# Three batches instead of four in the first output class, and four small moves in a two-layer mixture kernel

## The chip, the cores and the metric

The kernel runs on one core of one Trainium2 chip. The time is the device time of one execution, in microseconds (us); of several executions the median is given. On the core five engines work side by side, each with its own queue of instructions: TensorE (PE, matrix products; its weight loads are listed apart as PEld), VectorE (DVE), ScalarE (ACT), GpSimd (POOL) and SyncE (SP, which here issues nearly all DMAs). They wait for each other by semaphores.

## The reference, cut to what matters

```python
def kernel_reference(x, ...):                         # x: [8 batches, 256 tokens, 128]
    # layer 0: pooled = attention pooling of x, in 16 groups of 128 tokens
    logits = einsum('bld,ed->ble', pooled, gate_weight)              # 8 experts
    gates  = logits * (logits >= kth smallest of all logits)
    h = gelu_tanh(einsum('bld,ehd->bleh', pooled, w1) + b1)          # H = 512
    x = x + sum over e of gates_e * (einsum('bleh,edh->blde', h, w2) + b2)   # every token, every expert

    # layer 1, conditioning: one adapter for the language of each batch
    h = relu(x @ W1[lang] + b1[lang])                                # 128 -> 32
    z = x + h @ W2[lang] + b2[lang]                                  # 32 -> 128
    z = layernorm(z) * gamma[lang] + beta[lang]
    # layer 1, mixture: each token goes to 2 of 8 experts
    xn = layernorm(z) * gamma + beta
    w, idx = top_k(softmax(xn @ gate_w), 2);  w = w / sum(w)
    out = sum over its 2 experts of w_e * (gelu(xn @ w1_e + b1_e) @ w2_e + b2_e)
    return x + out + z
```

All of it is float32. There are 2048 tokens, 16 tiles of 128 (`NT = 16`); a batch is two tiles.

## The kernel before, in words

**Layer 0.** The tokens go in units, `UNITS = [(0,0,4), (1,0,4), (2,0,4), (3,0,2), (3,2,2)]`: group, offset and number of tiles. Units 0 to 2 have four tiles (`nt == GT`, 512 columns), units 3 and 4 two (256 columns). In `layer`, for each unit and expert, TensorE makes the hidden products `hp_first` (L945, four chunks, each evicted with the gelu by ScalarE, L947, into `hT_first`) and, one expert behind, the output products `yp_first` (L925). VectorE multiplies by the gates (`part_first`, L913) and adds up (`acc_first`, L915). Each product is 128 columns of weights, and as the operands are float32 each product takes two matmul records (passes) in a trace.

**The adapter and the routing of layer 1 run inside layer 0.** When the eighth expert of a unit is added up, `adapt(u, acc)` is queued in `behind`. It is a generator: `pump()`, called after each chunk of products (with 256 columns after every second), steps the first generator of the queue to its next `yield`. So where a product of `adapt` stands in TensorE's queue is set by the number of yields before it. In order, `adapt` does:

- `x2T`, the sum with x; `fp` (L566), transposes to rows of tokens, and `x2`;
- `adp` (L705): W1 of the adapter, two products, one for each half of the unit, into partitions 0 to 31 and `LANE` to `LANE + 31` of one tile (`LANE` is 64; `A` is 32); `ha` (L707): VectorE adds the bias, a column of the tile `las[u]`, and takes the relu, one operation for each half;
- `dp` (L715): W2, contracting over 33 rows (32 and a row of ones for the bias), alternating between the halves; `xr` (L720), the sum;
- the two layernorms (`normed`, with `ve` and `rstd` on VectorE and GpSimd), `zr`, the rows to be sent, `znp` (L749) transposes, and the gate: `l1q` (L763), the gate product in four blocks of 32 partitions, `l1p` (L770, L775);
- the top two by `top_one`, and `sofar`, running sums over the unit's tiles of how many tokens chose each expert (L802);
- `kp` (L808, L809): two products that turn the sums into each token's place among its expert's rows; then `at`, `wh`, `pos`, and GpSimd's indirect DMAs (L830), which scatter the tokens with their weights to the sorted rows `xs` in DRAM, eight for a unit of four tiles, four for one of two.

**The experts of layer 1.** Sorted rows go in tiles of 128, k = 0 to 35 (`SURE`) and up to three more under a runtime condition. After units 2, 3 and 4 a list (`listed`) says which tile holds which rows of which expert (`SLOTS = {2: 17, 3: 21, 4: 39}`): tiles 0 to 16 can begin once unit 2 is placed, 17 to 20 after unit 3, 21 on after unit 4. For a tile: `xt` is loaded, transposed (`xtp`, L1019, evicted as `xc`, L1021), the hidden products `hps` (L1034, gelu `hs`, L1036), output products `yps` (L1043), `yt` (L1047), which applies the token's weight, and an indirect DMA to `ys` (L1050). The last four tiles (`PLACED = 32` on) are not scattered: they are added for the last two batches by one-hot products `late` (L1106).

**The classes.** Within a list the tiles are sorted in three classes (`CLASSES`), by what their rows' batches are: those that hold rows of the first `FIRST = 4` batches come first, then those of the first `EARLY = 6`, then the rest. `holding` counts, from `kp`, how many tiles are full of the early ones. So the outputs of batches 0 to `FIRST - 1` are settled after tile `SETTLED_FIRST - 1` (k = 28) and those up to `EARLY - 1` after tile `SETTLED - 1` (k = 30); with

```python
SETTLED = max(SLOTS[NU - 2] + E, 4 * EARLY + E - 1)
SETTLED_FIRST = max(SLOTS[NU - 2] + E, 4 * FIRST + E - 1)
```

At these two tiles `load` brings the settled batches' rows of `ys` back (`yg`, L1069); the last two batches are loaded at the end. `add` makes two additions per batch (L1076, L1077) into `resid`, and `store` (L1085) sends them out.

**What sets the order.** The first part and the ending (from `manual_schedule` on) keep the written order on each engine; between them a scheduler orders by its own estimates, except what `keep_in_program_order` pins.

Of the kernel before, what the change touches and what calls it, by code (L numbers as in the profile page):

```python
# [10 lines left out]
F32 = mybir.dt.float32  # L11
# [3 lines left out]
ALU = mybir.AluOpType  # L15
# [7 lines left out]
B, S, D = 8, 256, 128  # L23
P = 128
NT = B * S // P
NG = 4
GT = NT // NG
# [3 lines left out]
NU = len(UNITS)  # L31
SLOTS = {2: 17, 3: 21, 4: 39}
E, HC = 8, 4
A = 32
LANE = 64
# [4 lines left out]
NSCR = 15  # L40
# [4 lines left out]
NSLOT = SLOTS[NU - 1]  # L45
SURE = 36
EARLY = 6
FIRST = 4
CLASSES = 3


# [33 lines left out]
def halves(u):  # L85

    g, o, nt = UNITS[u]
    b = (g * GT + o) // 2
    return (b, b + 1) if nt == GT else (b, b)
# [3 lines left out]
def tile_adaln_ffn_d2(ctx: ExitStack, tc: tile.TileContext, x, ptype, lang, cols, b1v,  # L93
                      w10, w20, w11d, w21d, lw1, lw2, lgb, out):
    nc = tc.nc
# [3 lines left out]
    const = ctx.enter_context(tc.tile_pool(name="const", bufs=1))  # L99
    first = ctx.enter_context(tc.tile_pool(name="first", bufs=E))  # L100
    keep = ctx.enter_context(tc.tile_pool(name="keep", bufs=NG))
    work = ctx.enter_context(tc.tile_pool(name="work", bufs=2))
    small = ctx.enter_context(tc.tile_pool(name="small", bufs=4))
    dram = ctx.enter_context(tc.tile_pool(name="dram", bufs=1, space=DRAM))
    psb = ctx.enter_context(tc.tile_pool(name="psb", bufs=4, space=PSUM))
# [36 lines left out]
    for e in range(E):  # L142
        t = first.tile([P, HC * P], F32, tag="w1", name=f"w10_{e}")
        nc.sync.dma_start(out=t, in_=w10[e])
        w10s.append(t)
        t = first.tile([P, HC, D], F32, tag="w2", name=f"w20_{e}")
# [16 lines left out]
    for i, (sign, keeps) in enumerate(((-1, ALU.is_ge), (1, ALU.is_ge), (1, ALU.not_equal))):  # L163
# [25 lines left out]
    lws, las, lgs = [], [], []  # L189
    langs = [nc.values_load(lgi[0:1, b:b + 1], engines=(SP,), min_val=0, max_val=NL - 1,  # L190
                            skip_runtime_bounds_check_because="a language's number") for b in range(B)]
    for u, (g, o, nt) in enumerate(UNITS):
        la = const.tile([LANE + A + 1, D + 1], F32, name=f"lw2_{u}")
        las.append(la)
        for i, b in enumerate(halves(u)):
            if nt == GT or not i:
                t = const.tile([P, A], F32, name=f"lw1_{b}")
                nc.sync.dma_start(out=t, in_=lw1[bass.ds(langs[b] * P, P), :])
                lws.append(t)
            nc.sync.dma_start(out=la[i * LANE:i * LANE + A + 1, :], in_=lw2[bass.ds(langs[b] * (A + 1), A + 1), :])  # L200
            if nt == GT or not i:
                t = const.tile([P, 2 * D], F32, name=f"lgb_{b}")
                nc.sync.dma_start(out=t, in_=lgb[bass.ds(langs[b], 1), :].rearrange("o w -> (o w)").partition_broadcast(P))
                lgs.append(t)
# [484 lines left out]
    def adapt(u, acc):  # L689
        g, o, nt = UNITS[u]  # L690
        n, t0 = nt * P, g * GT + o
        batches = range(t0 // 2, (t0 + nt) // 2)
        x2T = work.tile([P, GN], F32, tag="x2T", name=f"x2T{u}")[:, :n]
        nc.vector.tensor_tensor(x2T, acc, xT[g][:, o * P:o * P + n], ALU.add)
        yield
# [3 lines left out]
        yield  # L699

        m, lanes = n // 2, [slice(0, A), slice(LANE, LANE + A)]
        hp = psb.tile([LANE + A, S], F32, tag="big", name=f"adp{u}")[:, :m]
        ha = has[u % 2][:, :m]
        for i, b in enumerate(halves(u)):
            nc.tensor.matmul(hp[lanes[i], :], lhsT=lws[b], rhs=x2T[:, i * m:(i + 1) * m], start=True, stop=True)  # L705
        for lane in lanes:
            nc.vector.tensor_scalar(ha[lane, :], hp[lane, :], las[u][lane, D:D + 1], 0.0, ALU.add, ALU.max)  # L707
        yield
        yield

        dps = [psb.tile([P, 2, D], F32, tag="big", name=f"dp{u}_{i}") for i in range(2)]
        for t in range(nt // 2):
            for i, lane in enumerate(lanes):
                rows = slice(lane.start, lane.stop + 1)
                nc.tensor.matmul(dps[i][:, t, :], lhsT=ha[rows, t * P:(t + 1) * P], rhs=las[u][rows, :D],  # L715
                                 start=True, stop=True)
        z = work.tile([P, GT, D], F32, tag="xr", name=f"xr{u}")[:, :nt, :]
        for i in range(2):
            part = slice(i * nt // 2, (i + 1) * nt // 2)
# [83 lines left out]
        last[0] = sofar[:, nt, :]  # L803
        yield
        yield
        kp = pss.tile([P, GT + 1, E], F32, tag="sm", name=f"kp{u}")[:, :nt + 1, :]
        flat = kp.rearrange("p t e -> p (t e)")
        nc.tensor.matmul(flat, lhsT=one16, rhs=sofar.rearrange("p t e -> p (t e)"), start=True, stop=False)  # L808
# [7 lines left out]
            counts = small.tile([P, E], F32, tag="counts", name=f"counts{u}", bufs=2)  # L816
            nc.vector.tensor_copy(counts, kp[:, nt, :])
        for i, n0 in enumerate((FIRST, EARLY)):
            if t0 + nt == 2 * n0:
                some = small.tile([P, E], F32, tag="some", name=f"some{i}", bufs=1)  # L820
                nc.vector.tensor_copy(some, kp[:, nt, :])
                tiles_of(some, begun, f"some{i}", holding[:, i, :])
        for s, oh in enumerate((oh1, oh2)):
            wh = small.tile([P, GT, E], F32, tag="s", name=f"wh{u}_{s}")[:, :nt, :]
# [239 lines left out]
    of = out.rearrange("b (p u) d -> b p u d", u=2)  # L1064
    loaded = deque()

    def load(n, part, queue, group=None):
        y = work.tile([P, 2, 2 * D], F32, tag="scr", name=f"yg{n}_{part.start}", bufs=NSCR)[:, part, :]
        move = queue.dma_start(out=y, in_=yv[n, :, part, :])  # L1069
        if group:  # L1070
            tc.add_to_no_dep_group(group, move.ins)
        loaded.append((n, part, y))

    def add():
        n, part, y, o = taken_up()
        nc.vector.tensor_tensor(o, y[:, :, :D], o, ALU.add)  # L1076
        nc.vector.tensor_tensor(o, o, y[:, :, D:], ALU.add)  # L1077
        return n, o
# [5 lines left out]
    def store(queue, n, o):  # L1084
        queue.dma_start(out=of[n], in_=o)  # L1085
# [85 lines left out]
    store(nc.sync, *add())  # L1171
    placed.append(output(*hid.popleft()))
    brought(*placed[0], late, True)
    store(nc.sync, *add())
    placed.append(output(*hid.popleft()))
    for k in range(1, SURE - PLACED):
        brought(*placed[k], late, False, LATE * (k == SURE - PLACED - 1))
    for _ in range(FIRST, EARLY):
        store(nc.sync, *add())
    lasts = [add() for _ in range(LATE)]  # L1180
    for queue, (n, o), some in zip((nc.sync, nc.scalar), lasts, late):
# [60 lines left out]
```

## Time and profile before

| what | value |
|---|---|
| median of 6 runs | 353.02 us (351.2 to 353.93) |
| the profiled execution | 353.13 us, of which the span on the engines is 351.4 |
| mean granted TensorE clock | 0.987 |
| TensorE busy | 338.7 us, 96% of the span |
| VectorE, ScalarE, GpSimd busy | 198.2 (56%), 169.4 (48%), 93.9 us (27%) |
| longest idle of TensorE (before `yps` L1043, released by `xc` L1021) | 3.04 us |

A profile is one execution. Its page gives the busy time of each engine, the span in 40 slices (tenths busy, and the clock that TensorE was granted, 9 for nearly full), the chain of waits that ended last, and groups of instructions by line. The trace behind it gives a timeline (start, length, engine, line, operation, output <- inputs; in brackets the idle time of the engine just before and what released it), what each engine waited for, and the busy times of stretches. `PE` at 96% means that TensorE's queue is nearly the whole span; matmuls are pipelined, so the pitch from one start to the next tells what one costs, not its listed length.

### The profile page before, as it was taken

Reading aid. Unit: us, or ns where it says so; the run is one execution under the profiler, and the core shown is the slowest. Engines: PE = TensorE matmul, PEld = TensorE weight load, DVE = VectorE, ACT = ScalarE, POOL = GpSimd, SP = SyncE. Lnnn points to the kernel's source line nnn. Section 1 sums busy time; section 2 is a strip of 40 time slices with the busy share of each in tenths; the row PEclk is TensorE's granted clock in tenths of the full one; section 3 lists DMA queues with packets and bytes.
Section 4 is the critical chain, followed back from the end, with each engine's and each line's share of the span. In section 5 each row is a group of like instructions: output and inputs, shape, how many; then the busy total and the mean of one; then the engine's idle time right before and its main releaser. Section 6 shows DMA issues by size and latency. Waiting matters only on the chain. (4 is left out here: it accounts for less than half of the span.)

```text
span 351.4 us, 6117 instructions
## 1 busy us (share of the span) xinstructions
PE 338.7 (96%) x1662; PEld 223.8 (64%) x1662; DVE 198.2 (56%) x835; ACT 169.4 (48%) x393; POOL 93.9 (27%) x146
## 2 busy tenths in 40 slices
PE   7999999999999999999999999999999996999994
PEld 6784444444444444344444578877888996999993
DVE  3884755633045774655641268496787576523465
ACT  4574455435433344423334245542557763677660
POOL 6600000000000040452053003036132836455530
PEclk9999999999999999999999999999999999699998
DMA  6893599946122101130112011112574662477365
GB/s 190 256 322 74 137 366 382 379 150 185 54 89 90 62 30 60 53 70 30 31 60 60 15 32 30 48 46 62 155 206 148 202 188 85 144 228 209 112 198 181
DMA packets 35771, 47.56 MB, mean 135 GB/s; under 512 B 5449, under 2 KB 18588, under 8 KB 35736
## 3 DMA queue, kind: packets, MB, share of 16 engines
q1 hardware_dynamic: 32744, 42.17, 39.1%
q0 software_dynamic: 2144, 4.19, 3.5%
q10 hardware_dynamic: 848, 0.79, 0.8%
q8 instruction: 15, 0.25, 0.3%
q14 instruction: 20, 0.16, 0.2%
HBM read 32.66 MB, written 14.66 MB: 135 GB/s over the span
## 5 line engine op out<-in xcount | busy, mean ns | idle before, releaser
L947 ACT ACTIVATE hT_first<-hp_first,col 128x512 f32<-128x512 f32 (+1 forms) x160 | 92.5, 602 | 92.6 <-PE hp_first L945 79.6
L945 PE MATMUL hp_first<-poolT,w 128*128 128x512 f32 (+1 forms) x320 | 119.9, 512 | 0.5 <-ACT hT_first L947 0.5
L925 PE MATMUL yp_first<-hT_first,w 128*128 128x512 f32 (+1 forms) x320 | 120.1, 512 | 0.0
L945 PEld LDWEIGHTS hp_first<-poolT,w 128*128 128x128 f32 x320 | 58.6, 190 | 45.4 <-issue 40.2
L925 PEld LDWEIGHTS yp_first<-hT_first,w 128*128 128x128 f32 x320 | 58.6, 190 | 45.3 <-issue 41.2
L830 POOL DMA_INDIRECT xs<-zr,pos x32 | 32.5, 1015 | 67.0 <-DVE holding L653 32.7
L1036 ACT ACTIVATE hs<-hps,col 128x128 f32<-128x128 f32 x144 | 40.7, 377 | 16.4 <-PE hps L1034 6.1
L1043 PE MATMUL yps<-w,hs 128*128 x288 | 40.0, 285 | 3.3 <-ACT xc L1021 3.0
L1050 POOL DMA_INDIRECT ys<-yt,xt x32 | 32.2, 1005 | 31.0 <-DVE yt L1047 17.0
L913 DVE SCALAR_TENSOR_TENSOR part_first<-yp_first,col,gbc_first 128x512 f32<-128x512 f32 (+1 forms) x28 | 17.2, 615 | 40.8 <-PE yp_first L925 38.6
L1034 PE MATMUL hps<-xc,wt 128*128 128x128 f32 x288 | 39.6, 281 | 0.2 <-issue 0.2
L1043 PEld LDWEIGHTS yps<-w,hs 128*128 128x128 f32 x288 | 36.6, 199 | 3.8 <-issue 3.7
L1034 PEld LDWEIGHTS hps<-xc,wt 128*128 128x128 f32 x288 | 36.4, 197 | 0.8 <-issue 0.6
L1047 DVE SCALAR_TENSOR_TENSOR yt<-yps,xt,b 128x128 f32<-128x128 f32 x36 | 12.5, 348 | 24.3 <-PE yps L1043 18.7
L582 POOL TENSOR_TENSOR rstd_l<-ve_l,nhalf 128x4 f32<-128x4 f32 (+1 forms) x5 | 5.1, 1024 | 70.7 <-DVE ve_l L580 68.6
L1021 ACT ACTIVATE xc<-xtp,col 128x128 f32<-128x128 f32 x36 | 16.6, 472 | 9.7 <-PE xtp L1019 4.9
L915 DVE TENSOR_TENSOR acc_first<-acc_first,part_first 128x512 f32<-128x512 f32 (+1 forms) x35 | 20.1, 580 | 0.5
L516 POOL DMA_DIRECT2D gd_L<-gT_L x1 | 0.7, 660 | 61.1 <-DVE gT_L L514 61.1
L933 ACT ACTIVATE y_first<-yp_first,col 128x512 f32<-128x512 f32 x8 | 5.5, 687 | 23.2 <-PE yp_first L925 14.6
L1031 DVE TENSOR_TENSOR b<-b2all,xt 128x128 f32<-128x128 f32 x36 | 10.4, 289 | 8.0 <-issue 4.0
L531 DVE TENSOR_SCALAR_CACHE_REDUCE fl<-logit,tr 128x128 bf16<-128x128 f32 x46 | 13.5, 343 | 0.6
L550 DVE TENSOR_SCALAR_CACHE_REDUCE ok<-kt 128x3 f32<-128x3 f32 (+1 forms) x16 | 2.6, 160 | 13.8 <-PE kt L534 13.8
(253 smaller groups left out, 301.4 us busy)
## 6 DMA issues: line engine op xcount, KB each, us to landing
wt<-in_w_dram SPq DMA_DIRECT2D x36, 256.0 KB
xs<-empty SPq DMA_DIRECT2D x1, 8580.0 KB
w<-in_w_dram SPq DMA_DIRECT2D x24, 256.0 KB
gbc_first<-gd_L SPq DMA_DIRECT2D x24, 256.0 KB
xt<-xs SPq DMA_DIRECT2D x36, 65.0 KB
gbc_first<-gd_L SPq DMA_DIRECT2D x16, 128.0 KB
yg<-ys SPq DMA_DIRECT2D x8, 256.0 KB
xg<-in_x_dram SPq DMA_DIRECT2D x8, 128.0 KB
```

Source lines behind the costliest of these rows:

```text
L531: nc.vector.tensor_scalar(flags, lflat, values[:, i:i + 1], None, ALU.is_lt, ALU.add, accum_out=c[:, i:i + 1])
L830: move = nc.gpsimd.indirect_dma_start(out=xs, out_offset=bass.IndirectOffsetOnAxis(ap=pos[:, t:t + 1], axis=0), in_=zr[s][:, t, :], in_off ...
L913: nc.vector.scalar_tensor_tensor(part, y, bias, gbc, ALU.add, ALU.mult)
L915: nc.vector.tensor_tensor(accs[u], accs[u], part, ALU.add)
L925: nc.tensor.matmul(yp, lhsT=w2s[e][:, c, :], rhs=hT[:, c, :], start=(c == 0), stop=(c == HC - 1))
L945: nc.tensor.matmul(hp, lhsT=w1s[e][:, c * P:(c + 1) * P], rhs=sources[g][:, o * P:o * P + n], start=True, stop=True)
L947: nc.scalar.activation(hT[:, c, :], hp, act, bias=col[:, cb1 + e * HC + c:cb1 + e * HC + c + 1])
L1021: nc.scalar.activation(xc, tp, AF.Identity, bias=col[:, C_LB:C_LB + 1], scale=col[:, C_LG:C_LG + 1])
L1034: nc.tensor.matmul(hp[:, c, :], lhsT=wt[:, c * P:(c + 1) * P], rhs=xc, start=True, stop=True)
L1036: nc.scalar.activation(hT[:, c, :], hp[:, c, :], AF.Gelu, bias=b1all[:, bass.ds(number(k, ACT), 1), c])
L1043: nc.tensor.matmul(yp, lhsT=hT[:, c, :], rhs=w21[:, bass.ds(ek, 1), c * D:(c + 1) * D], start=(c == 0), stop=(c == HC - 1))
L1050: move = nc.gpsimd.indirect_dma_start(out=ys, out_offset=bass.IndirectOffsetOnAxis(ap=xt.bitcast(I32)[:, D:D + 1], axis=0), in_=yt, in_off ...
```

## The change

It does five things.

1. `FIRST` is 3 instead of 4: the first class holds the rows of three batches. Batch 3's rows are settled with batches 4 and 5, at k = 30; `SETTLED_FIRST` stays 29 (the first term of its maximum). As six tiles end inside unit 1, `holding` takes its count from the place `2 * n0 - t0` of `kp`. In the ending one more pair of additions and a store are written before the last tile's output, and one fewer after it.
2. All eight `yg` buffers are allocated at the first load.
3. In units of four tiles two more yields stand before `kp`.
4. In units of four tiles `adp` is made in four blocks of 32 partitions and 128 columns, and `ha` in four operations; for these the bias column is copied beside itself to the other 32 partitions of `las[u]`, two small pinned copies for each unit.
5. `dp` is made in the order second half, first half, with the second of a pair pinned behind the first, in the last unit both; so are the last unit's two `adp` products.

In TensorE's queue, `kp` thereby stands two 512-column products later in unit 0, four in unit 1, two 256-column ones in unit 2; unit 3's `adapt`, queued behind unit 2's, begins about four 256-column products (two records each) later; and the two `dp` products of unit 3, and of unit 4, stand side by side, where before a `yp_first` product or a transpose stood between. On SP the order of the loads and stores of the ending is the same but for batch 3's load, which comes with those of batches 4 and 5; on GpSimd the `rstd` of unit 4 stands behind one more scatter to `ys`.

```diff
--- before.py
+++ after.py
@@ -45,7 +45,7 @@
 NSLOT = SLOTS[NU - 1]
 SURE = 36
 EARLY = 6
-FIRST = 4
+FIRST = 3
 CLASSES = 3
 
 
@@ -190,14 +190,14 @@
     langs = [nc.values_load(lgi[0:1, b:b + 1], engines=(SP,), min_val=0, max_val=NL - 1,
                             skip_runtime_bounds_check_because="a language's number") for b in range(B)]
     for u, (g, o, nt) in enumerate(UNITS):
-        la = const.tile([LANE + A + 1, D + 1], F32, name=f"lw2_{u}")
+        la = const.tile([P, D + 2], F32, name=f"lw2_{u}")
         las.append(la)
         for i, b in enumerate(halves(u)):
             if nt == GT or not i:
                 t = const.tile([P, A], F32, name=f"lw1_{b}")
                 nc.sync.dma_start(out=t, in_=lw1[bass.ds(langs[b] * P, P), :])
                 lws.append(t)
-            nc.sync.dma_start(out=la[i * LANE:i * LANE + A + 1, :], in_=lw2[bass.ds(langs[b] * (A + 1), A + 1), :])
+            nc.sync.dma_start(out=la[i * LANE:i * LANE + A + 1, :D + 1], in_=lw2[bass.ds(langs[b] * (A + 1), A + 1), :])
             if nt == GT or not i:
                 t = const.tile([P, 2 * D], F32, name=f"lgb_{b}")
                 nc.sync.dma_start(out=t, in_=lgb[bass.ds(langs[b], 1), :].rearrange("o w -> (o w)").partition_broadcast(P))
@@ -690,6 +690,10 @@
         g, o, nt = UNITS[u]
         n, t0 = nt * P, g * GT + o
         batches = range(t0 // 2, (t0 + nt) // 2)
+        if nt == GT:
+            for i in (0, LANE):
+                tc.keep_in_program_order(
+                    nc.vector.tensor_copy(las[u][i + A:i + 2 * A, D + 1:], las[u][i:i + A, D:D + 1]))
         x2T = work.tile([P, GN], F32, tag="x2T", name=f"x2T{u}")[:, :n]
         nc.vector.tensor_tensor(x2T, acc, xT[g][:, o * P:o * P + n], ALU.add)
         yield
@@ -699,21 +703,35 @@
         yield
 
         m, lanes = n // 2, [slice(0, A), slice(LANE, LANE + A)]
-        hp = psb.tile([LANE + A, S], F32, tag="big", name=f"adp{u}")[:, :m]
+        hp = psb.tile([P, S], F32, tag="big", name=f"adp{u}")
         ha = has[u % 2][:, :m]
-        for i, b in enumerate(halves(u)):
-            nc.tensor.matmul(hp[lanes[i], :], lhsT=lws[b], rhs=x2T[:, i * m:(i + 1) * m], start=True, stop=True)
-        for lane in lanes:
-            nc.vector.tensor_scalar(ha[lane, :], hp[lane, :], las[u][lane, D:D + 1], 0.0, ALU.add, ALU.max)
+        if nt == GT:
+            for q in range(GT):
+                nc.tensor.matmul(hp[q * A:(q + 1) * A, :P], lhsT=lws[halves(u)[q // 2]], rhs=x2T[:, q * P:(q + 1) * P],
+                                 start=True, stop=True)
+            for q in range(GT):
+                i, j, quarter = q // 2, q % 2, slice(q * A, (q + 1) * A)
+                nc.vector.tensor_scalar(ha[lanes[i], j * P:(j + 1) * P], hp[quarter, :P],
+                                        las[u][quarter, D + j:D + j + 1], 0.0, ALU.add, ALU.max)
+        else:
+            for i, b in enumerate(halves(u)):
+                move = nc.tensor.matmul(hp[lanes[i], :m], lhsT=lws[b], rhs=x2T[:, i * m:(i + 1) * m],
+                                        start=True, stop=True)
+                if i or u == NU - 1:
+                    tc.keep_in_program_order(move)
+            for lane in lanes:
+                nc.vector.tensor_scalar(ha[lane, :], hp[lane, :m], las[u][lane, D:D + 1], 0.0, ALU.add, ALU.max)
         yield
         yield
 
         dps = [psb.tile([P, 2, D], F32, tag="big", name=f"dp{u}_{i}") for i in range(2)]
         for t in range(nt // 2):
-            for i, lane in enumerate(lanes):
-                rows = slice(lane.start, lane.stop + 1)
-                nc.tensor.matmul(dps[i][:, t, :], lhsT=ha[rows, t * P:(t + 1) * P], rhs=las[u][rows, :D],
-                                 start=True, stop=True)
+            for i in (1, 0):
+                rows = slice(lanes[i].start, lanes[i].stop + 1)
+                move = nc.tensor.matmul(dps[i][:, t, :], lhsT=ha[rows, t * P:(t + 1) * P], rhs=las[u][rows, :D],
+                                        start=True, stop=True)
+                if not i or u == NU - 1:
+                    tc.keep_in_program_order(move)
         z = work.tile([P, GT, D], F32, tag="xr", name=f"xr{u}")[:, :nt, :]
         for i in range(2):
             part = slice(i * nt // 2, (i + 1) * nt // 2)
@@ -803,6 +821,9 @@
         last[0] = sofar[:, nt, :]
         yield
         yield
+        if nt == GT:
+            yield
+            yield
         kp = pss.tile([P, GT + 1, E], F32, tag="sm", name=f"kp{u}")[:, :nt + 1, :]
         flat = kp.rearrange("p t e -> p (t e)")
         nc.tensor.matmul(flat, lhsT=one16, rhs=sofar.rearrange("p t e -> p (t e)"), start=True, stop=False)
@@ -816,9 +837,9 @@
             counts = small.tile([P, E], F32, tag="counts", name=f"counts{u}", bufs=2)
             nc.vector.tensor_copy(counts, kp[:, nt, :])
         for i, n0 in enumerate((FIRST, EARLY)):
-            if t0 + nt == 2 * n0:
+            if t0 < 2 * n0 <= t0 + nt:
                 some = small.tile([P, E], F32, tag="some", name=f"some{i}", bufs=1)
-                nc.vector.tensor_copy(some, kp[:, nt, :])
+                nc.vector.tensor_copy(some, kp[:, 2 * n0 - t0, :])
                 tiles_of(some, begun, f"some{i}", holding[:, i, :])
         for s, oh in enumerate((oh1, oh2)):
             wh = small.tile([P, GT, E], F32, tag="s", name=f"wh{u}_{s}")[:, :nt, :]
@@ -1064,8 +1085,12 @@
     of = out.rearrange("b (p u) d -> b p u d", u=2)
     loaded = deque()
 
+    brought_back = []
+
     def load(n, part, queue, group=None):
-        y = work.tile([P, 2, 2 * D], F32, tag="scr", name=f"yg{n}_{part.start}", bufs=NSCR)[:, part, :]
+        if not brought_back:
+            brought_back.extend(work.tile([P, 2, 2 * D], F32, tag="scr", name=f"yg{m}", bufs=NSCR) for m in range(B))
+        y = brought_back[n][:, part, :]
         move = queue.dma_start(out=y, in_=yv[n, :, part, :])
         if group:
             tc.add_to_no_dep_group(group, move.ins)
@@ -1171,11 +1196,12 @@
     store(nc.sync, *add())
     placed.append(output(*hid.popleft()))
     brought(*placed[0], late, True)
-    store(nc.sync, *add())
+    for _ in range(2):
+        store(nc.sync, *add())
     placed.append(output(*hid.popleft()))
     for k in range(1, SURE - PLACED):
         brought(*placed[k], late, False, LATE * (k == SURE - PLACED - 1))
-    for _ in range(FIRST, EARLY):
+    for _ in range(5, EARLY):
         store(nc.sync, *add())
     lasts = [add() for _ in range(LATE)]
     for queue, (n, o), some in zip((nc.sync, nc.scalar), lasts, late):
```

## The prediction

> **What bounds the kernel now.** I read the page first (busy shares, slices), then TensorE's timeline round every place the change touches, then the waits, then stretches of the second half.
>
> ```profile
> span 351.4 us, 6117 instructions
> PE 338.7 (96%) x1662; PEld 223.8 (64%) x1662; DVE 198.2 (56%) x835; ACT 169.4 (48%) x393; POOL 93.9 (27%) x146
> PEclk9999999999999999999999999999999999699998
> ```
>
> TensorE (PE) is busy in 96% of the span, so from the first gate products on only what shortens PE's own queue, or an idle PE, counts; what VectorE (DVE) or ScalarE (ACT) gain is hidden. The clock row has one dent (6, about 300 us), taken up below. Next PE's timeline; columns are start, length, engine, line, operation and, in brackets, idle time before and its releaser. Matmuls here are pipelined: I read pitches from starts, not lengths. A 512-column pass takes 0.43 us, a 256-column one 0.217.
>
> ```profile
> 116.82 0.38 PE L566 MATMUL fp<-ident,acc_first 128*128 128x128 f32 x2
> 117.14 0.63 PE L705 MATMUL adp<-x2T,lw 128*32 128x256 f32 x4
> 117.69 1.98 PE L925 MATMUL yp_first<-hT_first,w 128*128 128x512 f32 x4
> ...
> 137.19 0.43 PE L763 MATMUL l1q<-znT,col 128*32 128x128 f32 x8
> 137.55 1.12 PE L945 MATMUL hp_first<-poolT,w 128*128 128x512 f32 x2
> ...
> 141.63 1.45 PE L925 MATMUL yp_first<-hT_first,w 128*128 128x512 f32 x3
> 143.43 0.19 PE L808 MATMUL kp<-sofar,one 128*128 128x40 bf16 x1 [0.34 <-DVE sofar L802]
> ...
> 173.75 1.45 PE L925 MATMUL yp_first<-hT_first,w 128*128 128x512 f32 x3
> 175.55 0.19 PE L808 MATMUL kp<-sofar,one 128*128 128x40 bf16 x1 [0.35 <-DVE sofar L802]
> ...
> 238.77 0.48 PE L715 MATMUL dp<-lw,ha 33*128 33x128 f32 x2
> 239.19 0.70 PE L925 MATMUL yp_first<-hT_first,w 128*128 128x256 f32 x2
> 239.81 0.49 PE L715 MATMUL dp<-lw,ha 33*128 33x128 f32 x2
> 240.23 1.13 PE L925 MATMUL yp_first<-hT_first,w 128*128 128x256 f32 x4
> ```
>
> Four things to see. The adapter's first product in two blocks (adp, 128x256) holds PE from 117.14 to 117.69, 0.55 us. The gate product in four column blocks of the same 128*32 shape (l1q) does as many rows in 137.19 to 137.55, 0.36 us. The places' product (kp) comes 0.51 us late twice: 141.63 + 3 x 0.43 = 142.92 against 143.43, and 173.75 + 1.29 = 175.04 against 175.55; it waits for DVE's running sums. Unit 3's two dp products each run alone, 0.42 us each, a yp pair between them.
>
> Last the stretches (PE busy, PEld, DVE, ACT, POOL, granted clock, DMA share, GB/s):
>
> ```profile
> 291.50:295.00 3.50, 3.50 (x32) 3.45 (x32) 3.36 (x15) 0.20 (x1) 2.80 (x3) 1.00 0.29 95
> 295.00:298.50 3.50, 0.63 (x4) 0.27 (x2) 0.33 (x4) 0.99 (x5) 1.95 (x2) 0.95 0.18 57
> 298.50:302.00 3.50, 3.09 (x14) 3.12 (x15) 3.18 (x17) 3.17 (x11) 1.94 (x2) 0.50 0.24 54
> ```
>
> While POOL issues unit 4's scatters back to back, ACT gets no PE completion (it does 0.20 us of work in 3.5), PE runs dry for 3.04 us at 295.9 to 298.9, and then the clock is 0.50 until 305.0: 3.3 us idle and 3.4 lost to the clock, 6.7 in all. The change leaves this place as it is.
>
> **Part by part**, against the profiled 353.13 us (span 351.4, 1.7 outside it; 0.11 above the median 353.02).
>
> *Four blocks* (units 0, 1, 2). Per unit the same PE rows, in 0.36 instead of 0.55 us: 3 x 0.198 = 0.59 less. The other end is none, if the blocks did not overlap (4 x 0.112 for a 128-column pass is 0.45, with 0.1 of entry 0.55); l1q is the same shape, so I take its row. DVE pays: four ha operations of 0.34 (the 32x128 row) for two of 0.475, 0.41 us more. They lie between adp and dp; before, the last ha ends 118.83, 150.95 and 206.39 and dp starts 119.61, 151.72 and 207.19, so 0.77 us spare covers them and PE pays nothing. Without that cover it would be 0.41 each, 1.2 in all. The two bias copies are at most 0.17 each (the 128x15 rows): 1.0 us of DVE, which sits idle for tens of us over these units; none on the path.
>
> [...]
>
> *kp later by two yields.* Unit 0's kp moves two 512-column matmuls back (1.7 us), unit 1's four (3.4), unit 2's two 256-column ones: each more than the wait. Gains 0.51 + 0.51, and 0.15 in unit 2 (0.455 us of gap against 0.30 for an entry): 1.17; from 0.69 (the idle the profile names) to 1.25. What comes later behind it, POOL's scatters of these units, is needed by loads far behind. Unit 3's kp keeps its two yields and its 0.17: nothing. But all of unit 3's chain (fp, adp, dp, znp, kp, scatters) comes about eight passes, 1.74 us, later, as unit 2 takes longer.
>
> *dp pairs.* Unit 3's two come together: one run of 0.42 and one entry of 0.09 go, 0.50 less (0.4 to 0.7, as the entry before 239.81 is 0.19). Unit 4's also come together (before, 268.54 and 269.21, a transpose between them), the same 0.50, but unit 3's list work lies 1.74 us later on a DVE that is busy 5.08 of the 6.0 us from 264 to 270, in front of unit 4's x2 and ha. I place acc_7 at 265.3, fp 265.4, adp 266.3, yps 267.6, the dp pair 268.95 to 269.37: half is lost, 0.26 less (0.5 less to 0.5 more). (acc_7 is the last sum of unit 4's layer-0 output, from which fp is made.) Unit 4's norm starts 0.75 later; its lists are wanted by tile 21, whose rows landed 306.8 and were used at 311.15, 4.3 us of cover; with no cover it is 0.75 more.
>
> *First class and load buffers.* As many DVE operations, the same last class; the order of instructions on SP stays. The load of batch 3 moves behind the scatter of k = 30, and one more pair of additions (0.80 us) ahead of the last yt. The rows of that place:
>
> ```profile
> 339.70 2.15 SPq L1069 DMA_DIRECT2D yg<-ys  x4
> ...
> 343.65 0.35 DVE L1047 SCALAR_TENSOR_TENSOR yt<-yps,xt,b 128x128 f32<-128x128 f32 x1 [0.65 <-PE yps L1043]
> 343.91 0.41 DVE L1076 TENSOR_TENSOR resid<-yg,resid 128x256 f32<-128x256 f32 x1
> ```
>
> Before, four pairs follow the last yt on DVE, which then runs to 347.2; now three. If batch 4 lands at 343, up to 0.6 less. Of the two loads issued at 339.70 and 340.11 one landed 342.29, the other 344.71; with three in front of it batch 4 can be the late one, and then yt waits for it: up to 1.05 more. Neither end has the better row, so I take the middle, 0.2 more.
>
> Sum: -0.59 - 1.17 - 0.50 - 0.26 + 0.20 = -2.32: 350.81 profiled, **350.7** as a median. The ends added give -3.3 to -0.4, thus 349.7 to 352.6; misread pitches add some, so 349.0 to 352.3 is its own range.
>
> **Rivals.**
>
> *Held completions take a second bite* (slower). The dry spell at 295.9 is not the only one: at 239.4 to 245.2, beside unit 2's eight scatters, ACT sat idle 5.83 us for a PE completion, and PE escaped with 0.62 because 256-column work was queued. A like hold at 263 to 265.8 goes with unit 3's four scatters. These move 1.74 us later into unit 4's start, where PE waits for ACT and DVE at each step (fp, adp, dp). From about 3 us of dry PE on the clock halves too: 3.3 + 3.4 = 6.7 more, 350.8 + 6.7 = 357.5. A hold of 3 to 4 us without the clock makes 354.9. For it: scatters and holds go together three times of three. Against: at 263 PE lost nothing then, and eight passes more are queued.
>
> [...]
>
> *The gain is eaten* (no change). The late landing holds yt in full (+1.05) and unit 4's region costs +0.5 in place of -0.26: 350.8 + 0.85 + 0.76 = 352.4, with the two ha operations on the path 353.6.
>
> *The dry spell goes* (much faster). POOL's rstd of unit 4 comes one ys scatter later and the scatters' spacing shifts; if the completions come in time as at 263, 6.7 go: 344.1. For it: its size hangs on an alignment. Against: six runs of before lie within 351.2 to 353.9, so it is there each time.
>
> **Chances.** Forecast 0.55, eaten 0.13, dry spell gone 0.12, second bite 0.20 (0.12 at 357.5, 0.08 near 354.9). This kernel's measurement can tell about 0.5%, 1.77 us, from no change: faster is below 351.25, slower above 354.79. Of the forecast's 0.55 three quarters and a little more, 0.43, lie below 351.25. Faster 0.43 + 0.12 = 0.55, same 0.12 + 0.13 = 0.25, slower 0.20. The range takes in the gone dry spell (344.1) and goes up to 355.0, leaving out the full second bite and a little at each end.
>
> **What would show it.** adp 0.36 us in units 0 to 2, kp without idle time in brackets in units 0 and 1, four dp records in one group in units 3 and 4, batch 3's load at about 339.7, all confirm the sum; the idle 3.04 us before yps and the 0.50 clock should stand, some 2 us earlier. Wrong would be: an ha wait before dp, ACT idle "remote" round 262 to 270 with a second dent in the clock row, or the last yt waiting for batch 4.

## The result and the profile after

The changed kernel takes 354.96 us in the median (20 runs, 353.37 to 358.49), the kernel before 353.12 (46 runs). The ratio is 1.0069, with a 95% interval of 1.0050 to 1.0087: slower by 0.7%. The forecast was 0.65% faster. The time lies just inside the widest range given, which goes up to 355.0; the sign is wrong.

The profiled execution took 356.13 us, 1.2 above its own median, so its places count for more than its sum. The page of the changed kernel:

```profile
span 354.4 us, 6149 instructions
PE 336.8 (95%) x1674; PEld 223.9 (63%) x1674; DVE 200.6 (57%) x847; ACT 170.6 (48%) x393; POOL 92.3 (26%) x146
PEclk9999999999999999999999999999998999899997
```

TensorE is busy for less time (336.8 us against 338.7) in a longer span (354.4 against 351.4), so it stands idle more. First the places where the sum was right, in TensorE's timeline (columns as in the prediction):

```profile
117.61 0.43 PE L710 MATMUL adp<-x2T,lw 128*32 128x128 f32 x8
117.97 1.98 PE L946 MATMUL yp_first<-hT_first,w 128*128 128x512 f32 x4
119.89 0.72 PE L731 MATMUL dp<-lw,ha 33*128 33x128 f32 x8
...
144.91 0.18 PE L829 MATMUL kp<-sofar,one 128*128 128x40 bf16 x1
```

The four blocks hold TensorE for 0.36 us, as read off l1q; kp has no idle time in brackets any more; dp starts on its pitch although four ha operations now lie before it. Then the two places where it went wrong:

```profile
239.09 0.58 PE L731 MATMUL dp<-lw,ha 33*128 33x128 f32 x4
239.59 1.13 PE L966 MATMUL hp_first<-poolT,w 128*128 128x256 f32 x4
240.56 0.59 PE L946 MATMUL yp_first<-hT_first,w 128*128 128x256 f32 x2
242.89 1.13 PE L966 MATMUL hp_first<-poolT,w 128*128 128x256 f32 x4 [1.74 <-issue]
...
264.47 0.41 PE L566 MATMUL fp<-ident,acc_first 128*128 128x128 f32 x2
267.48 0.33 PE L1040 MATMUL xtp<-ident,xt 128*128 128x128 f32 x1 [2.60 <-DVE x L702]
267.74 0.41 PE L718 MATMUL adp<-x2T,lw 128*32 128x128 f32 x4
269.57 1.91 PE L1064 MATMUL yps<-w,hs 128*128 x8
```

At 241 TensorE stands 1.74 us, at 265 2.60. At the second place, a tile's transpose (xtp) has slipped between unit 4's fp and adp. The releaser in the bracket tells what it needs: VectorE's `x2` (shown as x), which frees the buffer that fp fills; in the kernel fp and xtp take turns in one pool of two buffers (`pss`, in PSUM, where the kernel puts TensorE's products). Eight yps records after it take 1.71 us (269.57 to 271.28) in place of 0.90: the granted clock is 0.50 there. What holds x2 is seen on VectorE and GpSimd in the same stretch:

```profile
263.87 0.96 POOL L851 DMA_INDIRECT xs<-zr,pos  x1 [0.30 <-issue]
265.13 1.03 POOL L851 DMA_INDIRECT xs<-zr,pos  x1 [0.30 <-issue]
267.00 0.42 DVE L702 TENSOR_TENSOR x<-fp,xg 128x256 f32<-128x256 f32 x1 [1.58 <-remote]
```

fp was through at 264.9, and VectorE heard of it at 267.0, after the last of unit 3's scatters. The trace's records of semaphore updates say the same of the first place: TensorE's own completions arrive at 239.43, 240.88, 242.30, 243.76 and 245.17, one in 1.4 us (only at 242.34 another follows closely), while the scatters start at 238.93, 240.20, 241.67 and 242.93. From 245.17 on, four come within 0.16 us. The records are not complete (443 updates for 518 instructions that make one), but ScalarE's starts bear them out:

```profile
242.37 0.47 ACT L968 ACTIVATE hT_first<-hp_first,col 128x256 f32<-128x256 f32 x1 [4.96 <-PE yp_first L946]
243.79 0.47 ACT L968 ACTIVATE hT_first<-hp_first,col 128x256 f32<-128x256 f32 x1 [0.95 <-PE hp_first L966]
245.24 2.32 ACT L968 ACTIVATE hT_first<-hp_first,col 128x256 f32<-128x256 f32 x6 [0.98 <-PE hp_first L966]
```

A third place lies in the ending. Batch 4's addition waits for its load with the last tile's yt behind it, and batch 6's waits once more:

```profile
345.45 0.42 DVE L1101 TENSOR_TENSOR resid<-yg,resid 128x256 f32<-128x256 f32 x1 [1.15 <-DMA yg<-ys]
345.91 0.43 DVE L1102 TENSOR_TENSOR resid<-resid,yg 128x256 f32<-128x256 f32 x1
346.16 4.27 SPq L1110 DMA_DIRECT2D out_dram<-resid  x7
346.26 0.34 DVE L1068 SCALAR_TENSOR_TENSOR yt<-yps,xt,b 128x128 f32<-128x128 f32 x1
...
347.92 0.43 DVE L1101 TENSOR_TENSOR resid<-yg,resid 128x256 f32<-128x256 f32 x1 [0.53 <-DMA yg<-ys]
```

A ledger helps more than two spans. It is the start of one and the same matmul, counted from the first hp_first, less that of the kernel before, in us; the columns further right belong to the experiments below. Each column is one profile, and not all come from one chip.

| up to | changed | yields in units 0, 1 only | the same, no pins on adp (2nd run) | before + yields in unit 2 (2nd run) |
|---|---|---|---|---|
| behind unit 0's adp | -0.20 | -0.20 | -0.20 | 0.00 |
| unit 2's layer done (229 us) | -1.64 | -1.64 | -1.64 | -0.01 |
| behind unit 2's scatters (246) | -1.03 | -2.87 | -2.87 | +3.09 |
| layer 0 done (263) | -1.10 | -2.82 | -1.83 | +3.02 |
| unit 4's dp done (272) | +2.07 | -0.33 | -1.48 | +6.89 |
| the last tile's hps (340) | +0.82 | -1.86 | -1.65 | +6.76 |

Of the 3.0 us between the two spans 0.5 lies before the first hp_first, where nothing was changed, 0.8 is the ledger's last row, and 1.7 is the ending: from the last tile's hps to the end it takes 13.25 us in place of 11.55. VectorE's two waits for loads there, 1.15 and 0.53, add up to as much.

### The profile page after: what moved, and what is told of

It is laid out like the page before. It is cut to its first block, busy times and chain, and to the rows that moved or that the text cites. A ratio compares the mean times of both kernels' runs of the same rounds, so it can differ in the third digit from the quotient of the medians.

```text
span 354.4 us, 6149 instructions
## 1 busy us (share of the span) xinstructions
PE 336.8 (95%) x1674; PEld 223.9 (63%) x1674; DVE 200.6 (57%) x847; ACT 170.6 (48%) x393; POOL 92.3 (26%) x146
## 5 line engine op out<-in xcount | busy, mean ns | idle before, releaser
L851 POOL DMA_INDIRECT xs<-zr,pos x32 | 31.7, 992 | 71.0 <-DVE x2T L698 17.2
L1040 PE MATMUL xtp<-ident,xt 128*128 128x128 f32 x36 | 9.9, 284 | 2.6 <-DVE x L702 2.6
```

Source lines behind the costliest of these rows:

```text
L851: move = nc.gpsimd.indirect_dma_start(out=xs, out_offset=bass.IndirectOffsetOnAxis(ap=pos[:, t:t + 1], axis=0), in_=zr[s][:, t, :], in_off ...
```

## The experiments

Theory H: the two extra yields in unit 2 put unit 3's adapter into unit 2's scatters and unit 3's own scatters over unit 4's start, where completions come late. Theory P: the pin on adp brings the waiting transpose forward. Rivals: the ending (T); the four blocks with their added VectorE work (B); completions that are late for a reason in VectorE's or ScalarE's own queues, and not for the scatters (C).

**The ending.** `FIRST` at 4 again in the changed kernel, and, the other way, at 3 in the kernel before, with the additions of the ending to match.

```diff
-FIRST = 3
+FIRST = 4
-    for _ in range(2):
-        store(nc.sync, *add())
+    store(nc.sync, *add())
-    for _ in range(5, EARLY):
+    for _ in range(FIRST, EARLY):
```

> The changed kernel with four batches in the first class again and the ending's additions as before. Theory T (the ending pays for the three batches: the last yt waits behind batch 3's and 4's additions, whose loads land late): from the start of the last tile's hps to the end of the span 11.5 us as before, where the changed kernel took 13.2; the median falls by 1.5 to 1.7 to about 353.3. Theory H (only the held completions at unit 4's start made it slower): the ending's length was luck of one profile, the median stays within 0.5 of 355.0. Under both the transpose of a tile's rows behind unit 4's fp still waits about 2.6 us for x2.

> The kernel before with three batches in the first class and the ending's additions of the change, nothing else. Theory T: 13.0 us from the last tile's hps to the end against 11.5, the median 1.5 above the kernel before, 354.6. Theory H: no change, 352.6 to 353.6. The waits for kp and the dry spell of 3.0 us near 296 stay as before under both.

Measured: 1.0077 (1.0048 to 1.0106), no better than the changed kernel, and 0.9993 (0.9974 to 1.0011). T falls as the cause. A small cost is not excluded: from the last tile's hps to the end the ten profiles with three batches take 11.9 to 14.4 us, 12.7 in the mean, the six with four 11.5 to 12.0, 11.8 in the mean. The times of the pairs do not show these 0.9 us, so that stays open.

The profile with four batches shows one thing more. At 263 its ledger is -1.11, where the changed kernel's is -1.10, and it has the same two waits (1.73 and 2.65 us). But behind the second the clock stays full, and at 272 its ledger is +0.50 in place of +2.07:

```profile
266.87 0.33 PE L1040 MATMUL xtp<-ident,xt 128*128 128x128 f32 x1 [2.65 <-DVE x L702]
267.13 0.41 PE L718 MATMUL adp<-x2T,lw 128*32 128x128 f32 x4
267.47 1.16 PE L1055 MATMUL hps<-xc,wt 128*128 128x128 f32 x8
268.47 1.06 PE L1064 MATMUL yps<-w,hs 128*128 x8
```

So the half clock, about 1.6 us there, comes in one execution and not in another. What decides is taken up below, under the rival's price.

**The yields.** The changed kernel with the yields before kp in units 0 and 1 only, and in none.

```diff
-        if nt == GT:
+        if u < 2:
             yield
             yield
```

> The changed kernel with the two extra yields before kp in units 0 and 1 only, so that unit 2's chain and unit 3's behind it stand as before. Theory H (unit 3's four scatters, 1.74 us later, hold back the completion of unit 4's fp): the 2.6 us wait for x2 falls under 0.5, the median to 352.0 to 352.6; kp of unit 2 waits 0.24 again. Rival B (the four blocks, their four ha operations and the bias copies delay unit 3's and 4's chain): the wait of 2.6 stays and the median is 355.0 or more.

> The changed kernel without the extra yields in any unit. Theory H: as with the yields in units 0 and 1 only, but 1.0 us of kp waits (0.51 twice) come back: about 353.2. Rival B: 356.0, the wait of 2.6 us for x2 stays.

Measured: 0.9971 (0.9947 to 0.9995) and 0.9994 (0.9962 to 1.0025), medians 352.65 and 353.35 against 353.30. Unit 2's two yields alone turn 0.7% slower (0.8% for the kernel with four batches, on this same chip) into 0.3% faster. The wait at 241 is gone. But the wait for x2 went only from 2.60 to 1.75:

```profile
262.69 0.41 PE L566 MATMUL fp<-ident,acc_first 128*128 128x128 f32 x2 [0.25 <-issue]
264.85 0.33 PE L1040 MATMUL xtp<-ident,xt 128*128 128x128 f32 x1 [1.75 <-DVE x L702]
265.11 0.64 PE L718 MATMUL adp<-x2T,lw 128*32 128x128 f32 x4
```

H named the larger part of the loss, but it expected under 0.5 here; the transpose is still in front of adp. Rival B falls: the four blocks stand in both kernels, and the median that it expected, 355.0 or more, did not come.

**The pin.** The kernel before with the last unit's adp pinned; and the changed kernel with yields in units 0 and 1 and no pins on adp.

```diff
+            if u == NU - 1:
+                tc.keep_in_program_order(move)      # in adp, kernel before
```

> The kernel before with nothing but the last unit's two adp products pinned in the written order. In TensorE's queue that puts a tile's transpose (xtp) between unit 4's fp and its adp, and brings its two dp products side by side. Theory P (that transpose needs the PSUM buffer which fp holds until VectorE has made x2, so TensorE stands still right behind fp): the transpose waits 0.5 to 1.0 us for x2, as fp ends 0.4 us before the held completions come through, dp saves 0.5; the median is 353.3 to 354.0. Theory H alone (only the place of unit 3's scatters matters, not the order): 352.8, no wait for x2 in TensorE's list of waits.

> The changed kernel with the extra yields in units 0 and 1 only and without the pins on adp: unit 4's adp and two hidden products stand before the transpose that waits for x2 again. Theory P with H: the wait of 1.9 us, which is left with the yields alone taken back, falls to about 1.0, and the half clock after it goes; the median falls from 352.65 to 351.2 to 351.9. Theory H alone: 352.65, the order changes nothing.

The pin alone makes the kernel before slower, 1.0032 (1.0014 to 1.0050), and its list of TensorE's waits has a line that was not there (total, times, longest, in us):

```profile
PE xtp L1021 <- DVE x L698: 1.1, 1, 1.1
```

Its profile does not show where the 0.3% lies, though: behind unit 4's dp its ledger is +0.08, at the last tile's hps +0.05, so there the wait is made up for (the two dp products now stand side by side). In the other kernel, without the pin, adp and half a tile's hps stand in front of the transpose, and cover 0.8 us of the wait:

```profile
263.99 0.41 PE L566 MATMUL fp<-ident,acc_first 128*128 128x128 f32 x2 [0.26 <-issue]
264.47 0.41 PE L718 MATMUL adp<-x2T,lw 128*32 128x128 f32 x4
264.82 0.71 PE L1053 MATMUL hps<-xc,wt 128*128 128x128 f32 x4
266.15 0.33 PE L1038 MATMUL xtp<-ident,xt 128*128 128x128 f32 x1 [0.62 <-DVE x L702]
```

Its ratio is 0.9971 (0.9948 to 0.9994), the same as with the pins. So P is shown for the wait, on both versions (1.1 us with the pin, 1.75 to 0.62 without); a cost in time is shown on the kernel before alone, and where it falls is open.

**The scatters.** The changed kernel without the scatters of units 3 and 4 (their tokens' rows are not sent; one run); and one with a GpSimd copy before each of them.

```diff
-            for t in range(nt):
+            for t in range(nt if u < 3 else 0):
```

> The changed kernel without the scatters of units 3 and 4 to the sorted rows (their tokens' rows are left out). Theory H (while GpSimd issues scatters back to back, TensorE's completions come through only one in 1.4 us): the wait of 2.6 us for x2 falls under 0.4, the dry spell of 3.1 us near 298 and the half clock behind it go; unit 2's hold at 241 stays with its 1.9 us; span 345 to 347. Rival C (the completions are late for another reason, VectorE's or ScalarE's own queues): waits of 2 to 3 us stay at both places, span 353 to 355.

TensorE's waits without the scatters:

```profile
PE xtp L1040 <- DMA xt<-xs: 2.0, 2, 1.5
PE hp_first L966 <- issue: 1.7, 1, 1.7
...
PE xtp L1040 <- DVE x L702: 0.9, 1, 0.9
```

The dry spell near 298, 3.13 us with half a clock behind it, is gone from the list (its stretch runs at 1.00 clock, TensorE 3.76 of 4.00 us busy); unit 2's wait, whose scatters are left, stays at 1.7; the wait for x2 falls to 0.9. Rival C falls: where the scatters are left out the waits of 2.60 and 3.13 us go, and where they are left in, beside unit 2, the wait stays. The wait of 0.9 us (under 0.4 was expected) is what is left of the transpose's wait for x2 with no scatter beside it; the order makes it. The span of 348.9 lies over the 345 to 347 expected; in the list waits of 2.0 us for tiles' rows are new.

> The changed kernel with a GpSimd copy of 128x128 before each scatter of units 3 and 4, which leaves 0.6 to 0.9 us between two scatters in place of 0.30. If held completions pass in the gaps (theory H with the gap as its size): the wait for x2 falls under 1.5 us, the dry spell near 298 under 2, the median to 350 to 353. If it is the time from the first scatter to the last that counts: the hold lasts 1.5 us longer at unit 3 and as much at unit 4, and the median is 356 to 358.

```diff
+                    rest_of = small.tile([P, 128], F32, tag="gap", name=f"gap{u}_{s}_{t}", bufs=2)
+                    tc.keep_in_program_order(nc.gpsimd.tensor_copy(rest_of, zr[s][:, t, :128]))
                 move = nc.gpsimd.indirect_dma_start(
```

Measured 1.0043 (1.0015 to 1.0070), 354.58 us. The transpose's wait falls to 1.04, and the dry spell breaks into one wait of 0.44 at 296 and two of 1.06 and 1.16 at 302 to 305, at full clock. But from 272 to 340 this kernel gains 1.0 us on the kernel before, and the changed one, with the dry spell, 1.25: what is gained at 296 is given back behind it. The waits fall as the first expectation has it; its median (350 to 353) did not come, nor did the second expectation's.

**Unit 2's and unit 0's and 1's yields, each alone on the kernel before**, and the gaps on the best version. These three fell on a chip on which the kernel before takes 346.60 us.

```diff
+        if u == 2:              # the other: u < 2
+            yield
+            yield
```

> The kernel before with two extra yields before kp in unit 2 alone. The scheduler then also sets unit 3's dp products side by side and puts the waiting transpose between unit 4's two adp products. Theory H (unit 3's chain, moved into unit 2's scatters and with its own scatters moved to unit 4's start): TensorE stands 1.5 to 2.5 us near 241 and 1.5 to 2.8 us for x2 near 265; with 0.24 (kp) and 0.5 (dp) gained the median rises by 1.0 to 2.5, to 354 to 355.5. Rival B (the four blocks with their four ha operations make the waits): neither wait, the median 0.5 lower, 352.5.

> The kernel before with two extra yields before kp in units 0 and 1 alone. The sum as predicted: kp's idle time of 0.34 and 0.35 us goes, 1.02 us less on TensorE up to unit 4; theory H: of it 0.3 to 1.0 is left at the end, since unit 4's fp then comes earlier against unit 3's scatters only as far as VectorE lets these come earlier too; the median 352.0 to 352.8.

> The best so far (the changed kernel, extra yields in units 0 and 1 only, no pins on adp) with a GpSimd copy of 128x128 before each of unit 4's four scatters, which are pinned. Theory H: the dry spell of 3.3 us with 3.4 us of half clock behind it breaks into two or three waits of 0.6 to 1.3 us at full clock, as with the gaps at units 3 and 4; the median falls from 351.8 to 349.5 to 351.0. If the later arrival of tile 21's rows eats this: a wait of over 1 us of a transpose for xt, and 351.5 to 352.5.

Measured: 1.0023 (0.9997 to 1.0048), 0.9979 (0.9960 to 0.9999) and 0.9947 (0.9925 to 0.9970). Unit 0's and 1's yields do what was predicted: their ledger is -1.04 at 229 us, and 0.7 us is left in the median. For unit 2's yields this chip was no test of the hold, since it has next to none: TensorE's completions at 243 come 0.43 us apart, beside scatters 1.3 to 1.5 apart, and the dry spell near 296 is absent in all three profiles (no idle time over 0.5 us between 286 and 305). That is where this chip is faster: the ledgers of its two profiles of the kernel before with yields fall by 6.6 and 6.7 us from 272 to 340, and the chip's time is 6.5 us lower. So the changed kernel, unit 2's yields alone and the best version, without the copies and with them, were run on one more chip:

> The changed kernel once more, beside the others on one chip. Where that chip holds TensorE's completions back during the scatters (the kernel before at 353): 0.5 to 0.9% slower than before, with waits near 241 and 265 of 1.7 to 2.8 us. Where it does not (the kernel before at 346.6, as in the last three comparisons): the predicted gains are left less the wait behind the pinned adp, 0.2 to 0.6% faster, with no wait near 241.

> The kernel before with two extra yields before kp in unit 2 alone, again. On a chip that holds completions back, theory H: 0.3 to 0.7% slower than before, TensorE stands over 1.5 us near 241 and over 1.5 us in all round unit 4's x2. On one that does not: within 0.3% of before, as in the first run. Rival B: 0.2% faster on both.

> The changed kernel, extra yields in units 0 and 1 only, no pins on adp. Holding chip: 0.3% faster than before as in its first run. Other chip: TensorE keeps all that it gained up to unit 4 (2.8 us), 0.5 to 0.9% faster.

> As the one before, with the GpSimd copies between unit 4's scatters. Holding chip: the dry spell of 3.3 us with its half clock breaks up, 0.5 to 1.2% faster than before and at least 0.3% faster than without the copies. Other chip: nothing to break up, within 0.2% of the one without the copies.

On this chip (before 354.30) the completions are held. The changed kernel: 1.0067 (1.0042 to 1.0091). Unit 2's yields alone: 1.0128 (1.0080 to 1.0177), 4.5 us of 354, about twice the upper end of what was expected; five of the six runs take 359.3 to 360.9 us, one 355.5. And the waits come with no four blocks in the kernel, so B falls here as well. The waits and the stretches from 241 (columns as in the prediction) show why:

```profile
PE hp_first L948 <- issue: 2.6, 1, 2.6
PE xtp L1022 <- DVE x L698: 1.9, 1, 1.9
```

```profile
241.00:244.50 3.50, 0.91 (x5) 0.45 (x3) 2.54 (x13) 0.47 (x1) 2.85 (x3) 1.00 0.52 95
244.50:247.00 2.50, 2.47 (x6) 2.00 (x7) 1.45 (x12) 0.86 (x3) 1.13 (x2) 0.55 0.08 27
```

TensorE stands 2.6 us, the clock is at 0.55 for the next 2.5 us, and 1.9 us follow at unit 4. With the yields there, the scheduler also sets the transpose between unit 4's two adp products without any pin. On the chip that does not hold completions the same kernel has no wait over 0.7 us at these places.

Best version: without the copies 0.9961 (0.9938 to 0.9984), with them 0.9953 (0.9932 to 0.9974). Each beats the kernel before on two chips, and the changed one beside which they ran on the last; that the copies add something is not shown (on the chip where nothing is held, no run without them was made). On the last chip they break the dry spell into waits of 1.07 and 1.16 us, but the clock is 0.50 from 303.4 to 306.8 all the same, and the 0.3% expected over the version without them did not come.

## Why the prediction was wrong

**Four blocks: right.** -0.20 us behind unit 0's adp, -0.6 for three, and no wait before dp; the cover of 0.77 us was there (unit 0: last ha ends 119.77, dp at 119.89, so 0.1 of it is left).

**kp in units 0 and 1: right.** With them alone the kernel before gains 1.04 us on TensorE (1.02 predicted).

**kp in unit 2: the step that failed.** The 0.15 did come, and somewhat more (the ledger goes from -1.64 to -1.89 behind this kp). But the prediction saw that all of unit 3's chain comes eight passes later and priced that only as list work on VectorE in unit 4, 0.26 less with ends of 0.5. It did not ask what this chain runs into first: unit 3's adp and dp move into unit 2's scatters, where the kernel before had lost only 0.62 us (243.35 + 8 x 0.217 = 245.09, and the next product starts at 245.71). There ScalarE sits idle for 4.96 us up to 242.37, hearing of one completion in 1.4 us, and TensorE's next hidden products wait for it. By itself, on the kernel before, the move costs 4.5 us on a chip that holds them.

**Unit 4's region: the second step that failed.** "fp 265.4, adp 266.3" assumed that adp follows fp; measured were 264.47 and 267.74. The order written by the pin and the scheduler has the transpose between, and the prediction priced the pinned pair without looking up which PSUM buffer each neighbour needs. It put this region at 0.26 less; in the profile the ledger rises by 3.2 there (-1.10 to +2.07). The pin by itself is 0.3% on the kernel before. "Its scatters later at unit 4's start" was the rival "held completions take a second bite", given 0.20, and priced at 354.9 without the clock; it came, twice in one run, and the clock with it.

**The rival's price.** It was put at about 3 us of dry TensorE before the clock halves, its author's estimate from one gap, the 3.04 us of the profile before. The changed kernel shows 2.60 us idle, then 0.57 of the clock over 268 to 272, where the kernel with four batches shows 2.65 us idle and then 1.00:

```profile
264.00:268.00 4.00, 1.30 (x11) 0.61 (x9) 2.42 (x14) 2.57 (x10) 1.86 (x2) 1.00 0.67 193
268.00:272.00 4.00, 4.00 (x25) 3.59 (x21) 2.78 (x19) 1.71 (x6) 0.00 (x0) 0.57 0.39 96
...
264.00:268.00 4.00, 1.35 (x11) 0.81 (x10) 2.34 (x15) 2.23 (x8) 1.46 (x2) 1.00 0.62 189
268.00:272.00 4.00, 4.00 (x37) 3.71 (x36) 3.20 (x22) 2.31 (x9) 1.01 (x1) 1.00 0.31 83
```

Gaps of 1.75 (yields in units 0 and 1 only: 0.50 from 265.6 to 268.2), 2.60, 2.63 (unit 2's yields alone, at 241), 3.04 and 3.13 us (the dry spells of the kernel before and the changed one) were followed by half clock here, while 1.74 (the changed kernel at 241), 2.44 (the changed kernel with the GpSimd copies, at 241) and 2.65 left it full. So the length of one gap does not decide. The traces show what goes with it: before the ending a half clock lasts 3.41 us or twice that (6.83 in the kernel before, from 298.17 to 305.00), and within a trace two of them begin a whole number of 3.41 us apart (268.52 and 302.65 in the changed kernel, ten; 244.76 and 272.07 with unit 2's yields alone, eight). If each trace is cut into pieces of 3.41 us on that grid, then from 60 to 335 us, in all 17 traces, each of the 18 pieces at full clock in which TensorE is busy 44% or less is followed by half clock, and none with 48% or more (26% ahead of the half clock of the kernel before; in the changed one 26% ahead of that at 302.65, and 51% at 241, where the clock stayed full). The gap of 2.60 us fell nearly whole into one piece (31% busy), the one of 2.65 us was shared by two (66% and 54%). So in these traces whether this rival's clock is paid hangs on where a gap lies on the grid, and that differed between these two.

**dp pairs: right in unit 3.** The pair holds TensorE for 0.50 us and its entry takes 0.20 (237.16 + 8 x 0.217 = 238.89 against 239.09), 0.70 in all; the two single ones took 0.42 each, with entries, reckoned in the same way, of 0.18 (236.85 + 8 x 0.217 = 238.59 against 238.77) and 0.19, 1.21. That is 0.51 less, as forecast (0.50). With the yields in units 0 and 1 only the pair takes 0.42, and the ledger falls by 0.61 there (-1.64 to -2.25).

**First class: its bad end came in the profile.** The sum took the middle, 0.2 more, between 0.6 less and 1.05 more for a yt that waits for a late load. In the profile batch 4's addition, ahead of the last yt, waits 1.15 us for its load, and the ending is 1.7 us longer. The times do not show that this class costs anything, as said above.

**The range.** Added as they stand, the ends of the parts give about 3.6 less to 0.5 more, not 3.3 to 0.4 less, and the sum's upper end was then drawn in from 352.6 to 352.3 where the text widens it; and a hold of 3 to 4 us on 350.8 makes 353.8 to 354.8, not 354.9. The measured time lies above all of these; it is near the 354.9 given for the rival without the clock, which is partly luck, as gains, two waits, half clocks and the ending add up to it.

**The dry spell.** "There each time" is wrong for one of the chips, where it is absent.

## What to carry to other kernels

A step that is moved later by a generator's yields moves all that is queued behind it too, and each product of that has to be laid beside what the other engines do at its new place, above all beside bursts of indirect scatters, which in this kernel, on the chips that held completions, cost TensorE little only where enough independent work was queued (0.62 us beside unit 2's scatters in the kernel before, 1.7 to 2.6 with the moves). A pin changes the neighbours of what it pins: look up for each new neighbour which buffer it waits for and who frees it (the pin on adp made a wait of 1.1 us in the kernel before). Where a kernel has room, put the products that other engines wait for outside such bursts (unit 2's yields alone, which put them there, made 354.3 us 4.5 longer), and leave work that needs no completion between a product and the next user of its buffer (adp and half a tile's hps there: a wait of 0.62 in place of 1.75).

## What the runs showed of the hardware

While GpSimd issued scatters back to back (0.30 us between them), TensorE's completions reached the other engines one or two at a time, about 1.4 us apart or more (in the changed kernel 239.43, 240.88, 242.30, 243.76 and 245.17; in the kernel before, the records at 240.81 and 244.36 are 3.6 apart), on the chips of the times near 353. A held stretch ended 1.5 to 2.4 us after the start of the last scatter of units 2 and 3 (in the changed kernel 242.93 to 245.17 and 265.13 to 267.0), and the completions held back then came within a few tenths of a microsecond (four from 245.17 to 245.33). With the scatters of units 3 and 4 left out, the wait for x2 was 0.9 us in place of 2.60, and the wait of 3.13 near 298 did not come. On one chip with the same kernels completions came 0.43 us apart beside the same scatters, and the kernel before took 346.6 us. Why the chips differ is open: nothing in the profiles names it. The clock's grid of 3.41 us, and the 44 and 48% on either side of its change, are told under the rival's price.
